# Attention logits from a shared ring of PSUM banks, two key tiles at a time

## The chip, the core and the metric

The kernel runs on one core of a Trainium2 chip. Five engines work in parallel, each through its own queue in order: TensorE (PE, matmuls, with PEld for the weight loads), VectorE (DVE), ScalarE (ACT), GpSimd (POOL) and SyncE (SP, which here only issues transfers). Matmuls write to PSUM[...]. The metric is the device time of one execution in microseconds (us); lower is better.

## The reference

The input is x, 8 images of 512 channels and 32 x 32 pixels, in float32. There are two residual layers. The second is a masked 1 x 1 convolution after a group norm. The first, which holds nearly all the work, is:

```python
t = cbs(x, cv1_w, cv1_bn, 0)                      # group norm before; 1x1 conv, batch norm, silu
ys = [t[:, :C], t[:, C:]]                         # C = 256
for i in range(2):
    z = cbs(ys[-1], m_cv1_w[i], m_cv1_bn[i], 1)   # 3x3 conv
    q, k, v = 1x1 conv of z                       # 4 heads of 64 channels, 1024 pixels
    logits = einsum('bhdi,bhdj->bhij', q, k + r) * 64 ** -0.5
    z = einsum('bhij,bhdj->bhdi', softmax(logits), v)
    ys.append(ys[-1] + silu(bn(conv1x1(z))))
x = x + cbs(concat(ys), cv2_w, cv2_bn, 0)
```

So each of 8 images passes twice through an attention over 1024 queries and 1024 keys with 4 heads.

## The kernel before

The attention is cut into 64 **units**: 8 images x 2 blocks x 2 pairs of heads (`hp`) x 2 halves of 512 queries. A unit has eight **key tiles** of 128 keys (`t`). Keys lie on the partitions, queries along the columns, and the two heads of a pair are the two halves of a [128, 2, 512] tile.

For each unit (class `Unit`, from line 412):

- `logits(t)` (L421): two matmuls, one per head, with 64 rows each (TensorE's tile 64*128), into the pair of banks `lg` of the pool `ps_l`; ACT copies the pair to `st` in one instruction of 1024 columns (L432); DVE keeps the running maximum `mx` (L436, L438).
- `top()` and `spread()` (L440, L449): transposes that turn the maxima into one negated maximum per query, spread over all partitions in `mb` (pool `ps_m`, two banks).
- `soften(t)` (L456): DVE adds `mb` to `st` (L458), ACT takes the exponential in place (L461), POOL sums the tiles (L464, L466).
- `values(t)` (L468): two matmuls, one per head, into 64 columns each (tile 128*64), accumulated over the eight tiles in `po` (pool `ps_o`, one bank).
- `finish()` (L480): denominators by a matmul with ones (L484, also 128*64), a reciprocal (L486) and a product (L487).

Units overlap: while unit u runs `soften` and `values`, the logits of the next unit, `nxt`, are computed, tile by tile. All else (3 x 3 and 1 x 1 convolutions, projections to q, k and v, norms) is written as generators, **fillers**, which yield after some two matmuls. Their results, and those of `top` and `finish`, go to single banks from `bank()` (L69), three of them in the pool `ps_f`. Eight banks in all: two for logits, two for `mb`, one for `po`, three for the rest.

The program order is set by the loop over **slots** of four units (one image and block): after each step of a unit, `advance(share)` (L886) runs fillers until a share of the slot's filler work is done. `slot_filler` (L781) lists this work with estimated times; what the next slot needs must be done after 0.74 of the steps. `clock.tick` adds estimates for the unit's own matmuls, which set only when delayed fillers (norms) are let in. A slot has 4 x 10.5 steps: per unit one after `top`, one after `spread`, eight tiles, and half a step after the last values. A list scheduler of the framework then places the instructions on each engine, by program order among those that it takes to be ready; pools hand out whichever buffer is free. So instructions can stand in another order than written.

The hand-written order within a unit is: `top`, fillers, `finish` of the unit before, `spread`, fillers; then per tile t: on even t from 2, the values of t-2 and t-1; the logits of the next unit's tile t; `soften(t)`, whose addition on DVE stands behind the next unit's maximum through a dependency that fixes only the order (`behind`); fillers. At the end the last two values.

Ten buffers of `st` (pool `stp`) hold the tiles of both units.

Of the kernel before, what the change touches and what calls it, by code (L numbers as in the profile page):

```python
# [17 lines left out]
ALU = mybir.AluOpType  # L18
AX = mybir.AxisListType
PSUM = bass.MemoryType.PSUM  # L20
IN_ORDER = mybir.DependencyInfo(mybir.DependencyClass.NoSync, mybir.DependencyReason.DATA)

P = 128
# [5 lines left out]
HALF = 512  # L29
# [3 lines left out]
KT = 8  # L33
# [6 lines left out]
def conv_preact_kernel(ctx: ExitStack, tc: tile.TileContext, x, cv1, cv2, mcv1, qkv, mcv2, bn, rw, rh, conv, s_in, t_in, out):  # L40
    nc = tc.nc
    stt = nc.vector.scalar_tensor_tensor

    def pool(name, bufs, **kw):
        return ctx.enter_context(tc.tile_pool(name=name, bufs=bufs, **kw))
# [12 lines left out]
    gr = pool("gr", 2)  # L58
    tp = pool("tp", 3)
    wt = pool("wt", 3)  # L60
    ps_l = pool("ps_l", 1, space=PSUM)
    ps_m = pool("ps_m", 1, space=PSUM)
    ps_o = pool("ps_o", 1, space=PSUM)
    ps_f = pool("ps_f", 3, space=PSUM)

    def pair(p, tag, name):
        return p.tile([P, 2, HALF], F32, tag=tag, name=name)

    def bank(name):  # L69
        return ps_f.tile([P, HALF], F32, tag="bank", name=name)  # L70
# [4 lines left out]
    def flat(t):  # L75
        return t.rearrange("p a b -> p (a b)")

    def load(dst, src):
        nc.sync.dma_start(out=dst, in_=src)  # L79
# [97 lines left out]
    class Image:  # L177
# [221 lines left out]
        def last(self, h, xn):  # L399
            n = self.n  # L400
            for cp in range(2):
# [6 lines left out]
                    nc.vector.tensor_tensor(res[:, c], ps, res[:, c], ALU.add)  # L408
                load(out[n, cp, :, :, ts(h, HALF)], res)


    class Unit:
        def __init__(self, im, i, hp, half):
# [7 lines left out]
        def logits(self, t):  # L421

            if t == 0:
                self.begin()
            lg = pair(ps_l, "lg", f"lg_{self.name}_{t}")
            for h in range(2):
                r = slice(HD * h, HD * h + HD)
                nc.tensor.matmul(  # L428
                    lg[:, h], self.k[r, ts(t, P)], self.q[r, self.hp, ts(self.half, HALF)], start=True, stop=True
                )  # L430
            st = pair(stp, "st", f"st_{self.name}_{t}")
            nc.scalar.copy(flat(st), flat(lg))  # L432
            self.st.append(st)
            if t == 1:
                self.mx = pair(one, "mx", f"mx_{self.name}")
                return nc.vector.tensor_tensor(flat(self.mx), flat(self.st[0]), flat(lg), ALU.max)  # L436
            elif t > 1:
                return nc.vector.tensor_tensor(flat(self.mx), flat(self.mx), flat(lg), ALU.max)  # L438

        def top(self):  # L440

# [11 lines left out]
                for c in range(4):  # L453
                    nc.tensor.transpose(self.mb[:, h, ts(c, P)], self.nm[:, h, c : c + 1].to_broadcast([P, P]), ident)  # L454

        def soften(self, t, behind=None):  # L456
            st = flat(self.st[t])
            add = nc.vector.tensor_tensor(st, st, flat(self.mb), ALU.add)  # L458
            if behind is not None:
                tc.add_manual_dep(add.ins, behind.ins.name, IN_ORDER, reason="maximum first")  # L460
            nc.scalar.activation(st, st, AF.Exp)  # L461
            if t == 1:
                self.acc = pair(one, "acc", f"sum_{self.name}")
                nc.gpsimd.tensor_tensor(flat(self.acc), flat(self.st[0]), st, ALU.add)  # L464
            elif t > 1:
                nc.gpsimd.tensor_tensor(flat(self.acc), flat(self.acc), st, ALU.add)  # L466
# [162 lines left out]
    units = [Unit(im, i, hp, half) for im, i in slots for hp in range(IT) for half in range(2)]  # L629
# [25 lines left out]
    clock = Clock()  # L655
# [118 lines left out]
    bg = Background()  # L774
# [6 lines left out]
    def slot_filler(s):  # L781

        prev = slots[s - 1] if s else (None, 0)
        nxt = slots[s + 1] if s + 1 < len(slots) else (None, 0)
        todo, needed = [], 0.0

        def add(us, g):
            nonlocal needed
            todo.append((us, g))
            needed += us  # L790

        im, i = nxt
        if im and i == 0:
            add(0.0, call(im.load_y))
        add(8.0, bg.take(8.0))
        if im and i == 1:
            add(7.0, im.conv_m2(0))
            add(9.0, bg.take(9.0))
        if prev[1] == 1:
            add(7.0, prev[0].conv_m2(1))  # L800
            add(0.0, call(lambda: bg.add(*(cls(prev[0], h) for cls in (Second, Last) for h in range(2)))))
        if im:
            add(32.0, im.conv3(i))
            add(7.0, bg.take(7.0))
            add(21.0, im.project(i))
        rest = SHARE - needed if im else 1e3
        if rest > 0:
            todo.append((rest if im else 84.0, bg.take(rest, wait=True)))
        total = sum(c for c, _ in todo)
        return needed, total, todo  # L810
# [37 lines left out]
    first, second = images[:2]  # L848
# [13 lines left out]
    positions(1)  # L862
    clock.run(bg.take(7.0, force=True))
    clock.run(first.project(0))
    for t in range(KT):
        units[0].logits(t)
        clock.run(bg.take(3.4))

    before = None
    for s in range(len(slots)):  # L870
        needed, total, todo = slot_filler(s)
        state = {"done": 0.0}

        def filler():
            for us, g in todo:
                start = state["done"]
                for cost in g:
                    clock.tick(cost)
                    state["done"] += cost
                    yield  # L880

                state["done"] = max(state["done"], start + us)

        fill = filler()

        def advance(share):  # L886
            goal = max(share * total, min(1.0, share / 0.74) * needed + 0.1)
            while state["done"] < goal:
                if next(fill, "end") == "end":
                    break  # L890

        steps = 4 * (KT + 2.5)
        for j in range(4):
            u = units[4 * s + j]
            nxt = units[4 * s + j + 1] if 4 * s + j + 1 < len(units) else None
            base = j * (KT + 2.5)
            u.top()
            clock.tick(0.9)
            advance((base + 1) / steps)
            if before:  # L900
                before.finish()
            u.spread()
            clock.tick(1.8)
            advance((base + 2) / steps)
            for t in range(KT):
                if t and t % 2 == 0:
                    u.values(t - 2)
                    u.values(t - 1)
                    clock.tick(2.0)
                top = None  # L910
                if nxt:
                    top = nxt.logits(t)
                    clock.tick(1.05)
                u.soften(t, top)
                advance((base + 3 + t) / steps)
            u.values(KT - 2)
            u.values(KT - 1)
            clock.tick(2.0)
            advance((base + KT + 2.5) / steps)
            before = u  # L920
        for _ in fill:
            pass
# [57 lines left out]
```

## Time and profile before

| what | value |
|---|---|
| time, median of 3 runs | 3639.33 us (3638.44 to 3651.5) |
| profiled execution, its own time | 3646.37 us |
| its span, first to last instruction | 3644.7 us |
| mean granted TensorE clock | 0.979 |
| busy PE / DVE / ACT / POOL | 93% / 57% / 47% / 32% |
| attention loop, first logits to last values | about 216 to 3540 us |

"L428" is line 428 of the kernel before. A row of a group gives engine, operation, output<-inputs, shapes, count, busy us and mean ns of one, then the idle time of the engine before them and what ended it. One matmul of the program in float32 appears as two in the profile, each with its weight load (PEld). 64*128, 128*64 and 128*128 are the part of the array that a matmul uses, rows by columns. Starts of weight loads show when the array took the next matmul; durations of matmuls overlap.

### The profile page before, as it was taken

The numbers are of one execution on the slowest core, as the hardware profiler recorded it, in microseconds if no ns is written. First come the engines' busy times: TensorE is split into PE (matmuls) and PEld (weight loads), VectorE is DVE, ScalarE is ACT, GpSimd is POOL, SyncE is SP. The second block draws the span as 40 slices with busy tenths as digits, with TensorE's granted clock in tenths as the row PEclk, the third lists the DMA queues.
The fourth block names the chain that finished last, engine by engine and source line by source line (L and its number), as shares of the span: only waits on it lengthen the run. The fifth ranks groups of instructions, "written<-read, shape, count | busy, mean of one in ns | idle before, by whom it ended". The sixth has DMA issues, their size and how long they took to land. (4 is left out here: it accounts for less than half of the span.)

```text
span 3644.7 us, 31236 instructions
## 1 busy us (share of the span) xinstructions
PE 3381.1 (93%) x11716; PEld 1464.6 (40%) x11716; DVE 2064.8 (57%) x2141; ACT 1722.7 (47%) x1801; POOL 1149.6 (32%) x523
## 2 busy tenths in 40 slices
PE   6899989998999999989999999989999999999988
PEld 3644334343434334343434344343434344343333
DVE  4435565465656565665656565665655565655542
ACT  3045764645454544534454534544455534544531
POOL 1003233233333323333333333333333323333330
PEclk9899999999999999999999999999999999999989
DMA  7652341320222241422223241423223141513345
GB/s 279 211 182 96 100 154 64 115 96 24 98 81 102 75 142 52 155 82 97 94 81 106 71 142 52 160 77 118 73 90 112 62 144 49 167 52 108 103 153 173
DMA packets 142279, 400.21 MB, mean 110 GB/s; under 512 B 13104, under 2 KB 14384, under 8 KB 142128
## 3 DMA queue, kind: packets, MB, share of 16 engines
q1 hardware_dynamic: 141408, 397.99, 32.7%
q8 instruction: 92, 1.51, 0.2%
q14 instruction: 59, 0.48, 0.0%
q10 hardware_dynamic: 720, 0.23, 0.0%
HBM read 318.47 MB, written 79.69 MB: 109 GB/s over the span
## 5 line engine op out<-in xcount | busy, mean ns | idle before, releaser
L466 POOL TENSOR_TENSOR sum<-sum,st 128x1024 f32<-128x1024 f32 x384 | 913.1, 2378 | 1143.2 <-ACT st L461 1140.6
L461 ACT ACTIVATE st<-st 128x1024 f32<-128x1024 f32 x512 | 540.3, 1056 | 882.3 <-DVE st L458 880.2
L438 DVE TENSOR_TENSOR mx<-mx,lg 128x1024 f32<-128x1024 f32 x384 | 468.1, 1219 | 783.6 <-ACT st L432 783.6
L432 ACT COPY st<-lg 128x1024 f32<-128x1024 f32 x512 | 512.8, 1001 | 428.9 <-PE lg L428 301.5
L428 PE MATMUL lg<-q,k 64*128 64x512 f32 x2048 | 614.5, 647 | 101.7 <-DVE mx L438 94.5
L472 PE MATMUL po<-st,v 128*64 128x512 f32 x2048 | 570.4, 631 | 72.3 <-ACT st L461 70.1
L458 DVE TENSOR_TENSOR st<-st,mb 128x1024 f32<-128x1024 f32 x512 | 618.9, 1210 | 4.8 <-PE mb L454 4.8
L241 PE MATMUL m<-plane,w_m 128*128 128x256 f32 x2304 | 574.2, 392 | 0.6 <-DVE dd L285 0.6
L241 PEld LDWEIGHTS m<-plane,w_m 128*128 128x128 f32 x2304 | 416.3, 190 | 243.9 <-issue 191.4
L172 PE MATMUL cv<-y,w_cv 128*128 128x512 f32 x1024 | 496.1, 615 | 4.3 <-DMA y<-y 4.3
L464 POOL TENSOR_TENSOR sum<-st,st 128x1024 f32<-128x1024 f32 x64 | 153.7, 2402 | 875.3 <-ACT st L461 856.2
L428 PEld LDWEIGHTS lg<-q,k 64*128 64x128 f32 x2048 | 163.6, 186 | 435.5 <-DVE mx L438 224.3
L172 PEld LDWEIGHTS cv<-y,w_cv 128*128 128x128 f32 x1024 | 180.4, 191 | 284.3 <-issue 274.6
L486 DVE RECIPROCAL rb<-den 128x512 f32<-128x512 f32 x64 | 214.9, 3357 | 121.6 <-PE den L484 121.5
L172 PE MATMUL cv<-x,w_cv 128*128 128x512 f32 x512 | 247.5, 623 | 14.5 <-ACT x L166 14.5
L472 PEld LDWEIGHTS po<-st,v 128*64 128x64 f32 x2048 | 103.8, 136 | 383.9 <-ACT st L461 240.5
L172 PE MATMUL l<-x,w_l 128*128 128x512 f32 x512 | 246.2, 617 | 7.9 <-ACT x L166 7.9
L172 PE MATMUL qk<-z,w_qkv 128*128 128x512 f32 x512 | 249.9, 613 | 0.5 <-DVE k L325 0.5
L131 ACT ACT_TABLE_LOAD x126 | 161.7, 1283 | 14.9 <-issue 9.7
L436 DVE TENSOR_TENSOR mx<-st,lg 128x1024 f32<-128x1024 f32 x64 | 78.0, 1219 | 148.1 <-ACT st L432 148.0
L461 ACT ACT_TABLE_LOAD x124 | 159.1, 1283 | 2.2
L172 PEld LDWEIGHTS cv<-x,w_cv 128*128 128x128 f32 x512 | 94.6, 196 | 151.0 <-issue 125.6
(143 smaller groups left out, 2301.8 us busy)
## 6 DMA issues: line engine op xcount, KB each, us to landing
w_m<-w_m SPq DMA_DIRECT2D x96, 768.0 KB, 4.3
w_cv<-in_cv SPq DMA_DIRECT2D x92, 512.0 KB, 3.5
y<-y SPq DMA_DIRECT2D x64, 512.0 KB, 4.8
x<-in_x SPq DMA_DIRECT2D x56, 512.0 KB, 4.8
y<-y SPq DMA_DIRECT2D x64, 256.0 KB, 3.4
k<-r SPq DMA_DIRECT2D x32, 512.0 KB, 3.8
res<-y SPq DMA_DIRECT2D x32, 512.0 KB, 4.5
xr<-in_x SPq DMA_DIRECT2D x32, 512.0 KB, 4.1
```

The costliest lines, as they stand in the source:

```text
L131: nc.scalar.activation(dst, src, AF.Silu, bias=bn_b[:, col : col + 1], scale=bn_s[:, col : col + 1])
L172: nc.tensor.matmul(ps, w, moving, start=(n == 0), stop=(n == len(terms) - 1))
L241: nc.tensor.matmul(ps[:, ts(co, 256)].rearrange("p (t x) -> p t x", x=F), w[:, co, c, dx], u[:, 9 * c : 9 * c + 8, dx : dx + F], start=(j ...
L428: nc.tensor.matmul(lg[:, h], self.k[r, ts(t, P)], self.q[r, self.hp, ts(self.half, HALF)], start=True, stop=True)
L432: nc.scalar.copy(flat(st), flat(lg))
L438: return nc.vector.tensor_tensor(flat(self.mx), flat(self.mx), flat(lg), ALU.max)
L458: add = nc.vector.tensor_tensor(st, st, flat(self.mb), ALU.add)
L461: nc.scalar.activation(st, st, AF.Exp)
L464: nc.gpsimd.tensor_tensor(flat(self.acc), flat(self.st[0]), st, ALU.add)
L466: nc.gpsimd.tensor_tensor(flat(self.acc), flat(self.acc), st, ALU.add)
L472: nc.tensor.matmul(self.po[HD * h : HD * h + HD], self.v[:, t, ts(h, HD)], self.st[t][:, h], start=(t == 0), stop=(t == KT - 1),)
L486: nc.vector.reciprocal(rb, den)
```

## The change

- The pools `ps_l` (a pair) and `ps_f` (three banks) become one: `ps_f` with five single banks, for logits, fillers, `top` and `finish`.
- `logits(t)` takes two single banks. ACT copies each head's half apart (512 columns), and DVE takes the maximum of each half apart.
- `in_turn` chains the maxima and the additions of `soften` on DVE in exactly the written order (an order alone, no wait across engines).
- Tiles go in pairs: the values of t-2 and t-1, `soften(t)`, the next unit's logits of t and t+1, `soften(t+1)`, then fillers for two steps.
- `finish` of the unit before moves behind `spread` and its fillers, right ahead of the first pair. The half step at the end is gone: 4 x 10 steps.
- The first unit's logits, ahead of the loop, go in pairs too.

```diff
-    ps_l = pool("ps_l", 1, space=PSUM)
-    ps_f = pool("ps_f", 3, space=PSUM)
+    ps_f = pool("ps_f", 5, space=PSUM)
...
+    def in_turn(instruction):
+        if turn:
+            tc.add_manual_dep(instruction.ins, turn.pop().ins.name, IN_ORDER, reason="order of the softmax")
+        turn.append(instruction)
...
-            lg = pair(ps_l, "lg", f"lg_{self.name}_{t}")
+            lg = [bank(f"lg_{self.name}_{t}_{h}") for h in range(2)]
...
-            nc.scalar.copy(flat(st), flat(lg))
             self.st.append(st)
+            for h in range(2):
+                nc.scalar.copy(st[:, h], lg[h])
             if t == 1:
                 self.mx = pair(one, "mx", f"mx_{self.name}")
-                return nc.vector.tensor_tensor(flat(self.mx), flat(self.st[0]), flat(lg), ALU.max)
-            elif t > 1:
-                return nc.vector.tensor_tensor(flat(self.mx), flat(self.mx), flat(lg), ALU.max)
+            for h in range(2 if t else 0):
+                so_far = self.st[0] if t == 1 else self.mx
+                in_turn(nc.vector.tensor_tensor(self.mx[:, h], so_far[:, h], lg[h], ALU.max))
...
-        def soften(self, t, behind=None):
+        def soften(self, t):
             st = flat(self.st[t])
-            add = nc.vector.tensor_tensor(st, st, flat(self.mb), ALU.add)
-            if behind is not None:
-                tc.add_manual_dep(add.ins, behind.ins.name, IN_ORDER, reason="maximum first")
+            in_turn(nc.vector.tensor_tensor(st, st, flat(self.mb), ALU.add))
...
-        steps = 4 * (KT + 2.5)
+        steps = 4 * (KT + 2)
...
-            base = j * (KT + 2.5)
+            base = j * (KT + 2)
             u.top()
             clock.tick(0.9)
             advance((base + 1) / steps)
+            u.spread()
+            clock.tick(0.9)
+            advance((base + 2) / steps)
             if before:
                 before.finish()
-            u.spread()
-            clock.tick(1.8)
-            advance((base + 2) / steps)
-            for t in range(KT):
-                if t and t % 2 == 0:
+                clock.tick(0.9)
+            for t in range(0, KT, 2):
+                if t:
                     u.values(t - 2)
                     u.values(t - 1)
                     clock.tick(2.0)
-                top = None
+                u.soften(t)
                 if nxt:
-                    top = nxt.logits(t)
-                    clock.tick(1.05)
-                u.soften(t, top)
-                advance((base + 3 + t) / steps)
+                    nxt.logits(t)
+                    nxt.logits(t + 1)
+                    clock.tick(2.0)
+                u.soften(t + 1)
+                advance((base + 4 + t) / steps)
             u.values(KT - 2)
             u.values(KT - 1)
             clock.tick(2.0)
-            advance((base + KT + 2.5) / steps)
```

More of the change, by code (lines that the diff above doesn't have):

```diff
@@ L409, in last @@
                 load(out[n, cp, :, :, ts(h, HALF)], res)
+    turn = []
+    def in_turn(instruction):
+        if turn:
+            tc.add_manual_dep(instruction.ins, turn.pop().ins.name, IN_ORDER, reason="order of the softmax")
+        turn.append(instruction)
     class Unit:
@@ L428, in logits @@
                 nc.tensor.matmul(
-                    lg[:, h], self.k[r, ts(t, P)], self.q[r, self.hp, ts(self.half, HALF)], start=True, stop=True
+                    lg[h], self.k[r, ts(t, P)], self.q[r, self.hp, ts(self.half, HALF)], start=True, stop=True
                 )
             st = pair(stp, "st", f"st_{self.name}_{t}")
-            nc.scalar.copy(flat(st), flat(lg))
             self.st.append(st)
+            for h in range(2):
+                nc.scalar.copy(st[:, h], lg[h])
             if t == 1:
                 self.mx = pair(one, "mx", f"mx_{self.name}")
-                return nc.vector.tensor_tensor(flat(self.mx), flat(self.st[0]), flat(lg), ALU.max)
-            elif t > 1:
-                return nc.vector.tensor_tensor(flat(self.mx), flat(self.mx), flat(lg), ALU.max)
+            for h in range(2 if t else 0):
+                so_far = self.st[0] if t == 1 else self.mx
+                in_turn(nc.vector.tensor_tensor(self.mx[:, h], so_far[:, h], lg[h], ALU.max))
         def top(self):
@@ L864, in conv_preact_kernel @@
     clock.run(first.project(0))
-    for t in range(KT):
+    for t in range(0, KT, 2):
         units[0].logits(t)
-        clock.run(bg.take(3.4))
+        units[0].logits(t + 1)
+        clock.run(bg.take(6.8))
     before = None
@@ L899, in conv_preact_kernel @@
             advance((base + 1) / steps)
+            u.spread()
+            clock.tick(0.9)
+            advance((base + 2) / steps)
             if before:
                 before.finish()
-            u.spread()
-            clock.tick(1.8)
-            advance((base + 2) / steps)
-            for t in range(KT):
-                if t and t % 2 == 0:
+                clock.tick(0.9)
+            for t in range(0, KT, 2):
+                if t:
                     u.values(t - 2)
```

## The prediction

> **What bounds the kernel now.** I read the busy shares first, then TensorE's timeline around the attention loop, then its weight loads (their starts show when the array accepts a matmul), then the groups of the two other engines.
>
> ```profile
> PE 3381.1 (93%) x11716; PEld 1464.6 (40%) x11716; DVE 2064.8 (57%) x2141; ACT 1722.7 (47%) x1801; POOL 1149.6 (32%) x523
> ```
>
> TensorE (PE) is the bound. But 93% busy says nothing of how well the time is used, so here are TensorE's matmuls in one stretch of the loop (start, duration, line, tiles, count):
>
> ```profile
> 1119.04 1.08 PE L472 MATMUL po<-st,v 128*64 128x512 f32 x4
> 1120.05 1.56 PE L241 MATMUL m<-plane,w_m 128*128 128x256 f32 x6
> 1121.55 1.13 PE L428 MATMUL lg<-q,k 64*128 64x512 f32 x4
> 1122.61 0.70 PE L241 MATMUL m<-plane,w_m 128*128 128x256 f32 x2
> 1123.31 1.08 PE L472 MATMUL po<-st,v 128*64 128x512 f32 x4
> 1124.32 1.56 PE L241 MATMUL m<-plane,w_m 128*128 128x256 f32 x6
> 1125.81 1.13 PE L428 MATMUL lg<-q,k 64*128 64x512 f32 x4
> ```
>
> Although the program writes the values of two tiles one after the other, each tile's values (L472, tile 128*64) and logits (L428, tile 64*128) stand alone between filler matmuls of the whole array (128*128): the list order puts a filler wherever the next piece isn't ready. Logits follow each other every 4.3 us, because there is one pair of banks for them and the chain logits 1.06, copy 1.00, maximum 1.22 (3.3 us with no waits between) must run before the next. What does a switch cost? The weight loads around one logits tile:
>
> ```profile
> 1506.64 0.19 PEld L172 LDWEIGHTS cv<-y,w_cv 128*128 128x128 f32 x1 [0.24 <-issue]
> 1507.07 0.19 PEld L172 LDWEIGHTS cv<-y,w_cv 128*128 128x128 f32 x1 [0.24 <-issue]
> 1508.02 0.30 PEld L428 LDWEIGHTS lg<-q,k 64*128 64x128 f32 x4 [0.76 <-issue]
> 1509.08 0.30 PEld L172 LDWEIGHTS cv<-y,w_cv 128*128 128x128 f32 x2 [0.76 <-issue]
> ```
>
> Fillers start 0.43 us apart, but the logits come 0.95 us after the last filler: 0.52 us lost on entry. The block then takes 1.06 us (1508.02 to 1509.08). And, near the end of the trace, one of only four places where the values of two tiles run together:
>
> ```profile
> 3503.16 0.20 PEld L472 LDWEIGHTS po<-st,v 128*64 128x64 f32 x4 [0.76 <-ACT st L461]
> 3503.64 0.14 PEld L472 LDWEIGHTS po<-st,v 128*64 128x64 f32 x2 [0.29 <-ACT st L461]
> 3504.07 0.14 PEld L472 LDWEIGHTS po<-st,v 128*64 128x64 f32 x2 [0.29 <-issue]
> 3505.03 0.30 PEld L172 LDWEIGHTS l<-x,w_l 128*128 128x128 f32 x2 [0.81 <-issue]
> ```
>
> Two tiles take 1.87 us here, against 2 x 1.01 = 2.02 apart (1119.04 to 1120.05 is one). So TensorE is busy, but pays for switching.
>
> [...]
>
> **The change part by part.** Counted through the timeline of weight loads, TensorE enters one of the small tilings (logits, values, denominators) from 128*128 work 873 times in all. The entry comes 0.95 us after the last load 412 times (after a 512-column filler: +0.52), about 0.52 us after 193 times (256 columns, which run 0.21 apart: +0.31), about 0.31 us after 100 times (128 columns, 0.11 apart: +0.20); the others are mixed with waits. Mean of these 705: (412 x 0.52 + 193 x 0.31 + 100 x 0.20) / 705 = 0.42 us.
>
> *Grouping.* If the new order is kept, a unit (64 of them: image, block, head pair, half) visits the small tilings five times: denominators with the first two logits, three times two values and two logits, and the last two values. 64 x 5 = 320 entries remain, 553 go: 553 x 0.42 = 232 us.
> *Second tile of a pair.* Two values together save 2.02 - 1.87 = 0.15 us; 256 pairs: 38 us. Two logits together aren't in the trace; bounded by nothing saved (2 x 1.06) and by 0.86 for the first tile as with the values (1.92), 0 to 0.20 us a pair. I take 0.20, since the streams are the same length: 51 us. Ceiling: 232 + 38 + 51 = 321 us.
> *How much of it comes.* A pair is adjacent only if all is ready. From the start of two logits: first tile out at about 1.1, first copy 1.7, four half maxima to 1.7 + 4 x 0.69 = 4.5, the second `soften` add to 5.7, its exp to 6.8. TensorE needs that exp after 1.92 (logits) + about 5 (filler for a fifth of a unit) + 0.94 (values of the first tile) = 7.9 us. The slack of 1 us is thin: an activation-table load (1283 ns in the page, 250 in all) uses it up. And the fourth unit of each group of four gets less filler. I take three quarters: 240 us.
> *Waits.* In the loop (216 to 3540 us), gaps between weight loads beyond 0.96 us add up to 207 us. Waits for the single pair of logits banks go (94.5 us by the waits of matmuls on mx L438), waits for five shared banks and the later exps come. I leave the sum as it is; the ends are -100 and +200.
>
> *Copies and maxima by half.* The rows that price it:
>
> ```profile
> L438 DVE TENSOR_TENSOR mx<-mx,lg 128x1024 f32<-128x1024 f32 x384 | 468.1, 1219 | 783.6 <-ACT st L432 783.6
> L408 DVE TENSOR_TENSOR x2r<-l,x2r 128x512 f32<-128x512 f32 x64 | 43.9, 686 | 78.1 <-PE l L172 72.0 <-DMA x2r<-x 6.1
> L338 ACT COPY v<-v 128x512 f32<-128x512 f32 x64 | 37.4, 584 | 41.0 <-PE v L330 40.1
> ```
>
> A maximum of 1219 ns becomes two of 686: +153 ns x 448 = 69 us of DVE. A copy of 1001 ns becomes two of 584: +167 ns x 512 = 86 us of ACT. Both are hidden behind TensorE: at 3400 us DVE would be (2065 + 69) / 3400 = 63% and ACT (1723 + 86) / 3400 = 53% busy. Without that cover the worst is the 69 us. The half copies also let the maximum of one half run beside the copy of the other.
> *The order on DVE.* add, four half maxima, add: 2 x 1.21 + 4 x 0.69 = 5.2 us in one fixed chain a pair. Behind a waiting maximum stand the second add, its exp, the values, and the release of the logits banks.
> *`finish` after `spread`.* The denominators move behind eight transposes and one portion of filler. Their wait for POOL's sums (17.5 us in all) goes. But reciprocal (3357 ns) and product (678 ns) now start with the first logits of a unit and delay the maxima of tile 1 to about 0.95 + 4.0 + 1.4 = 6.4 us after the denominators begin, and its exp to about 9 us; its values are due at 0.95 + 1.92 + 5 + 0.94 = 8.8. Break even; taken as nothing, the cost if not is about 64 x 1 us.
> No DMA is issued or removed; filler DMAs move with their filler, on the same SP queue.
>
> Sum, against the profiled execution's own 3646.4 us: 3646.4 - 240 = 3406. That execution is 7 us over the median of the runs, so **3400 us**.
>
> **Rivals.**
> *A, as above*: 3270 to 3490 (all of the ceiling with 50 us fewer waits, or half of it). Chance 0.53. For it: one pair of banks spaces the logits by 4.3 us today, and the new ring spaces two tiles by about 4.5.
> *B, the order breaks up again*: the second exp is late, the list order puts fillers between the two values and between values and logits, and a quarter of the ceiling comes: 3640 - 80 = 3560 (3500 to 3615). For it: today's order keeps only four of 256 pairs of values together. Against it: the distance grows from one tile to two. Chance 0.20.
> *C, slower: fillers starve for banks.* Fillers had three banks of their own; after two logits, four of five are taken. The first comes back at 1.7 + 0.69 = 2.4 us, and a filler of two matmul terms (1.72 us) needs its second bank at 1.92 + 1.72 = 3.6. That holds with 1.2 us to spare, but a reciprocal (3.36), a 2574 ns step of the convolution (L291) or a table load with its silu (1.28 + 0.78) in front of the copy or the maximum takes more. It decides from 240 / 256 = 0.94 us of extra wait a pair; at 2.4 us (every pair hit by one reciprocal-sized delay) the time is 3400 + 256 x 2.4 = 4010, at 1.5 us 3400 + 384 = 3784. I take 3780. Against it: in the 3324 us of the loop DVE is busy 1955 us and ACT 1655. Chance 0.22.
> *D, nothing changes*: saved switches are paid back in waits one for one: 3640. Chance 0.05, of which 0.04 within 0.5%.
>
> **How the numbers follow.** Half a per cent (18 us) is about what a measurement of this kernel can tell. Faster: A 0.53 + B 0.20 + the edge of D = 0.74; same 0.04; slower 0.22. The likeliest is A: 3400. About 0.06 of A lies below 3280; above 3690 lies most of C, some 0.14. So 3280 to 3690; A's own range is 3270 to 3490.
>
> **What would show it.** Values and logits in blocks of 16 weight loads (two tiles each) in the timeline; entries near 320 and not 873; two logits in about 1.92 us; DVE and ACT up by 69 and 86 us; logits' wait for mx gone. Wrong if pairs stand apart (B), or if filler weight loads wait for mx or for copies of the logits for more than some 250 us in all (C).

## The result and the profile after

The changed kernel takes 3577.93 us (median of 4 runs, 3576.06 to 3581.82) against 3640.46 us for the kernel before on the same chip: a ratio of 0.9824, 95% interval 0.9802 to 0.9845. It is faster by 62 us. The prediction said 240 us faster; the sign was right, the size nearly four times too large.

The page's busy shares of the changed kernel (busy us, share of the span, instructions):

```profile
PE 3333.1 (93%) x11716; PEld 1569.7 (44%) x11716; DVE 2144.3 (60%) x2589; ACT 1790.1 (50%) x2337; POOL 1160.5 (32%) x523
```

The share of TensorE is the same 93%. Its timeline in a good stretch of the changed kernel (start, duration, line, tiles, count) shows that the pairs formed:

```profile
331.96 1.94 PE L478 MATMUL po<-st,v 128*64 128x512 f32 x8
333.83 1.99 PE L435 MATMUL lg<-q,k 64*128 64x512 f32 x8
335.75 5.42 PE L171 MATMUL cv<-x,w_cv 128*128 128x512 f32 x12
341.10 1.94 PE L478 MATMUL po<-st,v 128*64 128x512 f32 x8
```

Values of two tiles take 1.87 us (331.96 to 333.83), logits of two 1.92 us (333.83 to 335.75): both as predicted. Counted through the weight loads, TensorE enters the small tilings 376 times instead of 873; the prediction had 320. So the main mechanism happened, and yet most of the gain is missing. A bad stretch, all engines but SP, shows one place where it went:

```profile
1034.52 1.08 PE L490 MATMUL den<-sum,ones 128*64 128x512 f32 x4
1034.89 0.78 ACT L130 ACTIVATE cv2s<-cv,bn_b,bn_s 128x512 f32<-128x512 f32 x1
1035.53 0.30 PEld L435 LDWEIGHTS lg<-q,k 64*128 64x128 f32 x4 [0.81 <-issue]
1035.53 2.97 PE L435 MATMUL lg<-q,k 64*128 64x512 f32 x8
1035.65 3.36 DVE L492 RECIPROCAL rb<-den 128x512 f32<-128x512 f32 x1 [3.17 <-PE den L490]
1036.07 0.19 PEld L435 LDWEIGHTS lg<-q,k 64*128 64x128 f32 x1 [0.24 <-issue]
1036.50 0.19 PEld L435 LDWEIGHTS lg<-q,k 64*128 64x128 f32 x1 [0.24 <-issue]
1036.75 1.56 ACT L441 COPY st<-lg 128x512 f32<-128x512 f32 x3 [1.08 <-PE lg L435]
1037.38 0.29 PEld L435 LDWEIGHTS lg<-q,k 64*128 64x128 f32 x2 [0.70 <-ACT st L441]
1038.44 0.30 PEld L171 LDWEIGHTS cv<-y,w_cv 128*128 128x128 f32 x2 [0.76 <-issue]
```

The first tile's four loads go together (1035.53): its two heads, of 64 rows each (64*128), run side by side, as the first experiment has it (1.06 us for both, 1.06 for one alone). Of the second tile, one head runs alone (1036.07, 1036.50), and the other waits until a copy of the first tile frees its bank (1037.38; which bank a tile gets is fixed in the program). Of the five banks, the denominators' is held by the reciprocal until 1039.01, and a filler's by its silu until 1035.67. The pair takes 2.91 us (1035.53 to 1038.44) instead of 1.92.

The groups that answer to those shown of before:

```profile
L441 ACT COPY st<-lg 128x512 f32<-128x512 f32 x1024 | 536.6, 594 | 477.5 <-PE lg L435 441.3
L446 DVE TENSOR_TENSOR mx<-mx,lg 128x512 f32<-128x512 f32 x768 | 482.1, 680 | 474.7 <-ACT st L441 474.6
```

And matmul waits (us in total, times, longest): two of the kernel before, then those of the changed kernel that answer to them, and three of its fillers' waits for maxima of the logits, which set their banks free:

```profile
PE lg L428 <- DVE mx L438: 94.5, 85, 3.7
PE po L472 <- ACT st L461: 70.1, 93, 3.4
...
PE po L478 <- ACT st L467: 42.4, 35, 3.3
PE lg L435 <- DVE mx L446: 31.3, 25, 4.1
PE cv L171 <- DVE mx L446: 15.8, 10, 2.9
PE m L240 <- DVE mx L446: 14.2, 12, 4.1
PE qk L171 <- DVE mx L446: 12.3, 21, 0.6
```

Half copies and half maxima cost 594 and 680 ns as expected. The waits of logits matmuls for maxima fell from 94.5 to 31.3 us.

One thing more is in the traces, and in neither the prediction nor its sum: half clock around and after long waits. TensorE starts its last weight load before a wait at 1111.74 us and the next at 1116.89; from 1115.5 to 1122.3 us only half of its clock is granted. The matmuls around the wait, and two stretches behind it (us; busy us of PE, PEld, DVE, ACT and POOL; granted clock; share and GB/s of DMA):

```profile
1111.68 1.08 PE L478 MATMUL po<-st,v 128*64 128x512 f32 x4
1116.89 2.07 PE L435 MATMUL lg<-q,k 64*128 64x512 f32 x2 [4.13 <-DVE mx L446]
...
1117.00:1122.00 5.00, 5.00 (x9) 2.91 (x10) 4.01 (x6) 2.40 (x3) 0.00 (x0) 0.50 0.29 108
1122.60:1125.60 3.00, 3.00 (x15) 2.62 (x15) 0.00 (x0) 1.05 (x1) 0.00 (x0) 1.00 0.41 158
```

At 0.50 the fillers' weight loads (L240) start 0.427 us apart, at 1.00 they start 0.216 us apart. Between the first logits and the last values the changed kernel has 28 such stretches, the kernel before 16, and each begins in a gap of over 2 us between weight loads or within 8 us after one. Half clock in that part adds up to 157 us, against 99.

### The profile page after: what moved, and what is told of

Its sections match the earlier page's. It is cut to its first block, busy times and chain, and to the rows that moved or that the text cites. A ratio compares the mean times of both kernels' runs of the same rounds, so it can differ in the third digit from the quotient of the medians.

```text
span 3580.1 us, 32601 instructions
## 1 busy us (share of the span) xinstructions
PE 3333.1 (93%) x11716; PEld 1569.7 (44%) x11716; DVE 2144.3 (60%) x2589; ACT 1790.1 (50%) x2337; POOL 1160.5 (32%) x523
## 4 chain that ended last, share of the span: by engine, by line
PE 68%; DVE 13%; issue 7%; ACT 7%; DMA 3%; POOL 2%; SPq 0%; ACTq 0%; POOLq 0%; DVEq 0%
PE cv L171 14%; PE lg L435 11%; PE po L478 10%; PE m L240 9%; PE qk L171 6%; PE l L171 6%; PE v L329 3%; DVE mx L446 3%; DVE st L466 2%; ACT st L441 2%; ACT st L467 2%; PE m L171 2%; PE den L490 2%; PE mt L454 2%; PE mb L462 1%
## 5 line engine op out<-in xcount | busy, mean ns | idle before, releaser
L441 ACT COPY st<-lg 128x512 f32<-128x512 f32 x1024 | 536.6, 594 | 477.5 <-PE lg L435 441.3
L446 DVE TENSOR_TENSOR mx<-mx,lg 128x512 f32<-128x512 f32 x768 | 482.1, 680 | 474.7 <-ACT st L441 474.6
L435 PE MATMUL lg<-q,k 64*128 64x512 f32 x2048 | 641.0, 632 | 43.0 <-DVE mx L446 31.3
L478 PE MATMUL po<-st,v 128*64 128x512 f32 x2048 | 536.4, 621 | 51.6 <-ACT st L467 42.4
L240 PE MATMUL m<-plane,w_m 128*128 128x256 f32 x2304 | 546.4, 391 | 19.0 <-DVE mx L446 14.2
L240 PEld LDWEIGHTS m<-plane,w_m 128*128 128x128 f32 x2304 | 437.6, 194 | 157.9 <-issue 47.1
L171 PE MATMUL cv<-y,w_cv 128*128 128x512 f32 x1024 | 476.3, 607 | 12.2 <-DVE mx L446 6.9
L435 PEld LDWEIGHTS lg<-q,k 64*128 64x128 f32 x2048 | 210.5, 188 | 458.8 <-issue 298.3
L492 DVE RECIPROCAL rb<-den 128x512 f32<-128x512 f32 x64 | 214.7, 3354 | 67.0 <-PE den L490 62.2
L171 PE MATMUL qk<-z,w_qkv 128*128 128x512 f32 x512 | 235.7, 603 | 12.3 <-DVE mx L446 12.3
L455 DVE TENSOR_REDUCE nm<-mt 128x4 f32<-128x512 f32 x128 | 82.5, 684 | 152.8 <-PE mt L454 152.8
```

The lines of the kernel that those rows point to most:

```text
L171: nc.tensor.matmul(ps, w, moving, start=(n == 0), stop=(n == len(terms) - 1))
L240: nc.tensor.matmul(ps[:, ts(co, 256)].rearrange("p (t x) -> p t x", x=F), w[:, co, c, dx], u[:, 9 * c : 9 * c + 8, dx : dx + F], start=(j ...
L435: nc.tensor.matmul(lg[h], self.k[r, ts(t, P)], self.q[r, self.hp, ts(self.half, HALF)], start=True, stop=True)
L441: nc.scalar.copy(st[:, h], lg[h])
L446: in_turn(nc.vector.tensor_tensor(self.mx[:, h], so_far[:, h], lg[h], ALU.max))
L478: nc.tensor.matmul(self.po[HD * h : HD * h + HD], self.v[:, t, ts(h, HD)], self.st[t][:, h], start=(t == 0), stop=(t == KT - 1),)
```

## The experiments

Times are medians of four runs, ratios against the kernel before on the same chip in the same batch.

| kernel | us | ratio (95% interval) | entries | logits blocks, us |
|---|---|---|---|---|
| before | 3640 to 3647 | 1 | 873 | 639 |
| the change | 3577.9 | 0.9824 (0.9802-0.9845) | 376 | 697 |
| written order, 5 banks | 3589.7 | 0.9853 (0.9828-0.9878) | 322 | 719 |
| ring alone | 3623.7 | 0.9934 (0.9913-0.9955) | 741 | 733 |
| order alone | 3673.8 | 1.0077 (1.0059-1.0094) | 749 | 666 |
| 7 banks | 3466.8 | 0.9512 (0.9486-0.9537) | 345 | 590 |
| 3 weight buffers, 5 banks | 3574.0 | 0.9808 (0.9784-0.9832) | 376 | 693 |
| written order, 7 banks | 3495.7 | 0.9588 (0.9557-0.962) | 322 | 522 |
| written order, 2 pairs + 3 | 3593.6 | 0.9861 (0.9833-0.9888) | 322 | 530 |
| 7 banks, additions first | 3324.7 | 0.9116 (0.9091-0.9142) | 325 | 532 |
| 5 banks, additions first | 3545.1 | 0.9716 (0.9692-0.974) | 370 | 689 |
| old loop, 2 pairs + 3 | 3673.0 | 1.0069 (1.0043-1.0095) | 783 | 725 |
| 5 banks, denominators early | 3547.2 | 0.9717 (0.9688-0.9746) | 429 | 665 |
| 7 banks, additions first, denominators early | 3313.2 | 0.9082 (0.9068-0.9095) | 388 | 531 |
| 5 banks, both | 3535.2 | 0.9681 (0.9659-0.9702) | 409 | 666 |

The batches differ by a few us, so runs of different batches are best compared by their ratios. Entries are counted in TensorE's order. "Logits blocks" is the time from the first weight load of each run of logits to the next load of anything else, summed over the trace; a wait of whatever comes behind a block counts in. Without losses I estimate it from the first experiment: 2048 loads x 0.2145 us (a quarter of the 0.858 us of a tile's streaming) plus 0.2 us at the end of each block: 546 us for before (536 blocks), 504 for the change (324 blocks).

### The price of a visit by itself

The new kernel in outline (its own code is longer; it was run once):

```diff
+ for width in (512, 256): for stage in "abcdegh": repeat 16 times
+     3 fillers; (h: logits of one head); 3 fillers
+     (e, g: values of one tile); (d, e, g: values of one tile)
+     (b, c, g: logits of one tile); (c, g: logits of one more); (h: the other head)
```

> This kernel computes none of the reference: it repeats matmul streams 16 times each, in fixed order, to price a visit to the small tilings by itself. Stages: a six fillers; b six fillers and the logits matmuls of one tile; c two tiles of logits; d values of one tile; e values of two; g values of two and logits of two; h three fillers, one head's logits, three fillers, the other head's. First with fillers of 512 columns, then of 256. Theory 1 (a visit is cheap[...]): over stage a, per repetition with 512 columns, b about 1.27 us, c 2.1, d 1.2, e 2.1, g 4.0; with 256 columns b about 1.27. Rival (the price in the prediction is right): b 1.58, c 2.44, d 1.53, e 2.39, g 4.3; with 256 columns b 1.37. For h, both heads alone: about 2.5 us, twice b, if a head alone takes as long as both together.

TensorE's timeline in stage b with fillers of 512 columns, in stage b with 256, and in stage h:

```profile
122.32 5.42 PE L58 MATMUL fwb<-xa 128*128 128x512 f32 x12
127.67 1.13 PE L58 MATMUL lg<-xa 64*128 64x512 f32 x4
128.73 5.42 PE L58 MATMUL fwb<-xa 128*128 128x512 f32 x12
...
862.78 1.13 PE L58 MATMUL lg<-xa 64*128 64x512 f32 x4
863.84 2.86 PE L58 MATMUL fnb<-xa 128*128 128x256 f32 x12
866.63 1.13 PE L58 MATMUL lg<-xa 64*128 64x512 f32 x4
...
770.79 1.12 PE L58 MATMUL lg<-xa 64*128 64x512 f32 x2
771.85 2.84 PE L58 MATMUL fwh<-xa 128*128 128x512 f32 x6
774.62 1.12 PE L58 MATMUL lg<-xa 64*128 64x512 f32 x2
```

A repetition of stage b is 6.41 us (122.32 to 128.73). Fillers' loads alone start 0.429 us apart, twelve take 5.15. So a logits tile in between costs 1.26 us, not 1.58. Likewise, over the fillers: two tiles of logits 2.12, values of one 1.21, of two 2.07, values of two and logits of two 3.98, and in stage h 2.50, each as theory 1 had it. With 256 columns a repetition of b is 3.85, its twelve fillers 2.59 (0.216 each): again 1.26. The weight loads show where the difference lies: the first load of the fillers comes 0.95 us after the last logits load, but the second only 0.11 us later, not 0.43. The trace shows these times and not the reason for them. The kernel before agrees without this experiment: in its trace, entries without a long wait come 0.42 us late on average, as the prediction counted, and the second load after a block comes 0.20 us ahead of the regular spacing.

For the streaming of a tile of four loads I take 0.858 us, two spacings of the fillers (2 x 0.429); a second tile adds as much, of logits (2.12 - 1.26 = 0.86) and of values (2.07 - 1.21 = 0.86). With v for a visit, l and w for the end of a block of logits or values: v + l = 1.26 - 0.86 = 0.40, v + w = 0.35, v + l + w = 3.98 - 3.43 = 0.55. So v = 0.20, l = 0.20, w = 0.15 us.

Stage h tells the other price: one head alone takes 1.06 us (770.79 to 771.85), as long as both heads together (127.67 to 128.73). A tile whose heads stand apart between fillers costs 2.50 instead of 1.26.

### What the prediction assumed, in full

Every matmul and transpose of TensorE goes through this:

```diff
+    def pe(instruction):
+        if pe_turn:
+            tc.add_manual_dep(instruction.ins, pe_turn.pop().ins.name, IN_ORDER, reason="written order")
+        pe_turn.append(instruction)
```

> The changed kernel with every TensorE matmul of the loop held to the written order (order alone). TensorE then enters the small tilings 322 times and the two heads of a tile never stand apart, which is what the prediction assumed in full. Prediction's prices: 320 us under the kernel before, near 3325, if the waits stay at some 207 us. Theory 1 (entry worth 0.2 us, and not 0.42): 110 + 89 = 200 us, so 3440 with unchanged waits, and later by whatever waits grow since nothing may step forward; I expect 3440 to 3560. Theory 2 (the order is irrelevant, the gain came from five banks): like the changed kernel, 3580.

3589.7 us: no faster than the list order (3577.9), above theory 1's range, and near theory 2's number, though not for its reason. With 322 entries and 256 blocks of two tiles, the logits blocks take 719 us, 229 over their price: 125 of these lie inside the blocks, and 103 pass before the filler behind a block can start. Gaps between weight loads, from the first logits to the last values, exceed 0.96 us by 270 us in all, against 207 in the changed kernel. Perfect pairs are worth little while banks aren't free.

### Ring alone, order alone

For the first, the loop of the kernel before with the new `logits`; for the second, the new loop with

```diff
-    ps_f = pool("ps_f", 5, space=PSUM)
+    ps_f = pool("ps_f", 3, space=PSUM)
+    ps_l = pool("ps_l", 1, space=PSUM)
...
-            lg = [bank(f"lg_{self.name}_{t}_{h}") for h in range(2)]
+            lg = pair(ps_l, "lg", f"lg_{self.name}_{t}")
```

and full-width copies and maxima.

> Five single shared banks, copies and maxima by head and the fixed DVE order, but the loop of the kernel before, tile by tile (TensorE order: 741 entries against 873 before and 376 after). Theory 1 (the gain is the fewer visits): 132 entries by 0.2 us less, more tiles with their heads apart (78 against 27), so 3610 to 3660. Theory 2 (the gain is the ring, no longer waiting for one pair): about 3580.

> The new loop in pairs of tiles with the old banks: one pair for logits, three for fillers, copies and maxima at full width (TensorE order: 749 entries). Theory 1: the pairs can't form with one pair of banks, 124 entries by 0.2 us less, 3600 to 3640. Theory 2 (the ring is the gain): 3640. If it is at 3580, the new places of the additions and of the denominators are what counts, and neither ring nor visits.

The ring alone gains 0.7%, in theory 1's range: its logits blocks are the longest of the table (733 us; 78 tiles have their heads apart in the order, against 27 before and 54 in the changed kernel). The order alone loses 0.8%, which no theory had. Its matmul waits, with one pair of banks under a loop that asks for two:

```profile
PE lg L436 <- DVE mx L446: 112.5, 72, 4.9
PE mt L454 <- DVE mx L446: 34.9, 19, 3.3
```

Neither part does what both do together. 55 of its tiles have their heads apart in the order, although both share a pair of banks: it is the list order that parts them there.

### Seven banks

```diff
-    wp = pool("wp", 4)
+    wp = pool("wp", 3)
...
-    ps_m = pool("ps_m", 1, space=PSUM)
...
-    ps_f = pool("ps_f", 5, space=PSUM)
+    ps_f = pool("ps_f", 7, space=PSUM)
...
-            self.mb = pair(ps_m, "mb", f"mb_{self.name}")
+            self.mb = pair(one, "mb", f"mbs_{self.name}")
             for h in range(2):
+                mb = bank(f"mb_{self.name}_{h}")
                 for c in range(4):
-                    nc.tensor.transpose(self.mb[:, h, ts(c, P)], ...)
+                    nc.tensor.transpose(mb[:, ts(c, P)], ...)
+                nc.scalar.copy(self.mb[:, h], mb)
```

> The changed kernel with seven banks in the ring: the spread maxima go through two ring banks into SBUF (two ACT copies of 584 ns a unit), which frees their two banks; three weight buffers instead of four pay for the space. The list order has 345 entries (376 with five banks). Theory 1 (with five banks the second head's logits wait for a bank of their own, and the two heads, which else run side by side, run one after the other; the logits blocks took 697 us, 193 over the price of the separate streams): the blocks fall by 100 us or more and the time to 3440 to 3500. Rival (banks aren't short; what is lost is lost to the late exponentials): 3560 to 3600.

> Control for the run with seven banks: the changed kernel with three weight buffers and five banks; TensorE's order is the same. All theories: 3575 to 3600.

3466.8 us against 3574.0 for the control: two more banks are worth 107 us, with 345 entries against 376 (the way of the spread maxima through SBUF comes with them and was not run by itself). The logits blocks fall from 693 to 590 us, by 103: 73 us inside them, 45 at the fillers behind them, while waits of values behind them grow by 18. This is theory 1's case, with the fillers' own waits for banks as a second part of it. Elsewhere the time between blocks falls by 55 us and that of the denominators by 12, while the values blocks grow by 61, so it is by chance that the 103 and the 107 are so close. What grows are values waiting for exponentials (seven banks):

```profile
PE po L479 <- ACT st L468: 124.4, 86, 3.8
PE po L479 <- DVE q L494: 16.6, 14, 3.2
```

against 42.4 us in the changed kernel.

> Seven banks and every TensorE matmul in the written order: 322 entries, heads never apart in the order. Theory 1: logits blocks near their price (some 500 us against 719 with five banks in the written order), waits for exponentials stay or grow by some 70 us: 3400 to 3470. Rival (lost to late exponentials, not to banks): 3560 to 3600, as with five banks in the written order.

> Seven banks split: two pairs for the logits of two tiles, full-width copies and maxima, three single banks for fillers, and the written order. Both heads of a tile share one pair, so neither waits alone. Theory 1: logits blocks near 500 us; fewer banks can be lent between logits and fillers, DVE and ACT are 155 us less busy: 3400 to 3480. Rival (sharing one ring matters): clearly slower than the written order with seven single banks, by over 40 us.

In the written order, seven banks bring 3589.7 down to 3495.7; the logits blocks come to 522 us, near their price, and the values' waits for exponentials rise to 178.6 us. That is a little above theory 1's range and well under the rival's. Split into two fixed pairs and three filler banks, the same seven banks give 3593.6: the logits blocks are as good (530 us), but 98 us are lost elsewhere. The values blocks are the same too (703 us against 701), so most of it, 87 us, lies between the blocks, among the fillers: gaps of over 0.96 us take 68 us more over the regular spacing there, and loads at half clock 15 more. A part are waits of fillers for the results of others to leave the three banks, in rows which the run with one ring doesn't have:

```profile
PE qk L419 <- DVE k L324: 15.1, 14, 1.5
PE m L419 <- ACT m2s L130: 14.2, 7, 2.9
```

So sharing one ring matters, as the rival to that run had it; these two rows are 29 us, and the rest is spread over smaller ones.

### The additions first

```diff
                 u.soften(t)
+                u.soften(t + 1)
                 if nxt:
                     nxt.logits(t)
                     nxt.logits(t + 1)
                     clock.tick(2.0)
-                u.soften(t + 1)
```

> Seven banks, and both additions of a pair ahead of its logits' maxima on DVE. Theory 1 (with banks enough, what remains are the values waiting for exponentials that stand behind four half maxima; 124 us of matmul waits on the exponential with seven banks): the second exponential comes some 2.8 us sooner, the waits fall by 60 us or more, 3370 to 3420. Rival (ACT itself is late, busy with copies and table loads): 3450 to 3480.

> The changed kernel (five banks) with both additions of a pair ahead of the maxima. The additions hold the logits banks 1.2 us longer. Theory 1 (banks are what is short with five): little or nothing, 3550 to 3600, and logits blocks as long as before or longer. Rival (the late exponential is the main loss in the changed kernel too): under 3520.

With seven banks: 3324.7 us, 142 us less, more than theory 1 said. The matmuls' waits on the exponential, of seven banks with additions first:

```profile
PE po L479 <- DVE q L494: 19.3, 19, 3.8
PE po L479 <- ACT st L468: 17.0, 14, 3.0
```

From 124.4 to 17.0 us; the logits blocks fall too, to 532, since the list order now keeps 247 of the pairs whole (206 with seven banks alone). With five banks the same edit brings some 1.1% (0.9716 against 0.9824), slightly more than expected, while the logits blocks stay at 689 us: the late exponential is a second loss, beside the banks and smaller while they are short.

### More banks for the old loop

The kernel before with `ps_l` of two pairs and the maxima through SBUF.

> The kernel before, tile by tile, with a second pair of logits banks (maxima through SBUF, three weight buffers); order with 783 entries. Theory 1 (bank waits and visits both count): the waits for the one pair go (some 95 us of matmul waits), the visits stay: 3540 to 3600. Rival (more banks do all of it, pairing tiles nothing): near the 3467 of seven banks with pairs.

3673.0 us, 0.7% slower: a miss of both. The waits for the pair are all but gone (6.3 us), but they come back as waits for exponentials:

```profile
PE po L473 <- ACT st L462: 149.0, 126, 5.1
```

(70.1 before). The order falls into 783 entries with 95 tiles' heads apart. A second pair of banks alone does nothing for a loop that works tile by tile. A ring of seven single banks under the old loop was not run.

### The denominators' place

```diff
+            if before:
+                before.finish()
+                clock.tick(0.9)
             u.spread()
             clock.tick(0.9)
             advance((base + 2) / steps)
-            if before:
-                before.finish()
-                clock.tick(0.9)
```

> The changed kernel with the denominators back ahead of the spread maxima (429 entries against 376). The prediction took the move as nothing. Theory 1: 53 entries by 0.2 us and the old wait for POOL's sums, 10 to 30 us slower than the changed kernel: 3585 to 3610. If the delayed maxima behind the reciprocal cost more than that, it is faster: under 3565.

3547.2 us, 1.1% faster than the change although it has 53 entries more. The logits blocks fall from 697 to 665 us. Two causes were left: the denominators' bank, held through the reciprocal, or the reciprocal in front of the maxima on DVE.

> Seven banks, additions first, and the denominators back ahead of the spread maxima. Theory 1 (the denominators' bank, held through the reciprocal of 3.36 us, is what their late place costs with five banks): with seven banks the place doesn't matter, 3315 to 3345, or a little slower for more entries. Rival (the reciprocal in front of the first pair's maxima is the cost): 3285 to 3305.

> Five banks, additions ahead of the maxima, and the denominators back ahead of the spread maxima. Alone the two gave some 33 us each over the changed kernel. Theory 1 (they mend different things): about 3510 to 3525. Rival (both mend the first pair's late exponential): about 3545.

With seven banks and the additions first, the old place brings 3313.2 against 3324.7, by the ratios 0.3%, and the intervals touch. With five banks and the additions first it brings 3535.2 against 3545.1, again 0.3 to 0.4%, and again the intervals touch. Without the additions first, five banks gave 1.1%. So once the additions are first the place is worth the same with five banks as with seven, and these runs don't decide between the two causes. For the bank: the early place shortens the logits blocks with five banks, by 32 us and with the additions first by 22, and with seven not at all (532 and 531). For the reciprocal in front of the maxima: putting the additions first takes most of the gain away. That the bank is held while a head waits, the excerpt from 1034.52 us shows; what share of the 1.1% it has stays open, and so does whether the two reorderings add up (3535.2 lies between the two expectations). The version with seven banks, additions first and early denominators is the fastest: 0.9082 of the kernel before (0.9068 to 0.9095).

## Why the prediction was right and wrong

**Grouping** formed as foreseen: 376 entries for 320 predicted. **The step that failed first is "553 x 0.42 = 232 us"**: the visit was mis-sized. The 0.42 us is what is lost on entry, and the prediction didn't look at what is gained back on exit. Its own excerpt showed it, the two loads at 1509.08 that stand as one row. Measured, a visit costs 0.20 us, for wide and narrow fillers alike. 497 entries fewer are 99 us.

**The second tile**: 0.15 and 0.20 us a pair were right. Not all pairs are whole: logits blocks fell from 536 to 324, values blocks from 511 to 336, which is 42 + 26 us.

**"How much of it comes", three quarters**, put the shortfall down to exponentials; these cost 42.4 us of matmul waits, less than the 70.1 before, though putting the additions first did gain 1.1%. **The second step that failed is the term on waits, "waits for five shared banks and the later exps come. I leave the sum as it is"**: the waits for the shared banks got no number. The time in logits blocks over their price rose from 92 to 193 us. Inside the blocks it rose from 29 to 126 us, where a head or a tile waits for its banks (as at 1037.38) or the heads stand apart in the order (54 tiles, 27 before). Before the filler behind a block it rose from 3 to 55 us. Before values that follow directly it fell from 61 to 12 us. That the banks are at the root of it, the runs in the written order show: no heads are apart in the order there, and 229 us over the price with five banks become 32 with seven.

**Waits** of the old kind were left at 207 us, and the gaps in the loop of the changed kernel come to 207 us too, but they are others: over the whole trace those at entries fell by 55 us (75 to 20), and those between whole-array loads rose by 30 (38 to 68).

Put together from the two traces: -99 (visits) - 42 - 26 + 2 (block ends of logits, values, denominators) - 55 + 30 (waits) + 100 + 14 + 10 (logits, values and denominators over their price) = -66 us. The spans differ by 3644.7 - 3580.1 = 64.6. That it closes so well is partly chance: whole-array loads at half clock, which the sum leaves out where a gap is under 0.96 us, cost 22 us over their regular spacing before and 45 after, so a term may well be off by 20 us. Some of the long waits inside blocks stand in the last terms, so the split between waiting and running apart is not exact.

**Copies and maxima by half**: the durations add up to 95 us more for the copies (86 predicted) and 62 more for the maxima (69). DVE is at 60%, ACT at 50%, so there is room to hide them; no run prices them by themselves. The maximum of one half does run beside the copy of another: in the good stretch above, the four copies of a pair start at 335.17 us and take 2.02, and their maxima start at 335.76.

**`finish` after `spread` at nothing** was wrong: some 1% of the time. The working had the reciprocal's and the product's 4 us on DVE and called it break even, and left out that the denominators' bank is one of the five for all of the reciprocal (3354 ns). Which of the two is the larger part isn't settled.

**The rivals.** C named the right resource and half of the victims: fillers' matmuls do wait for maxima of the logits, by some 54 us (15.8 + 14.2 + 12.3 + 7.0 + 4.2, rows cv, m, qk, v, m of the waits), but this is far from C's threshold of 0.94 us a pair, 240 us. The logits' own second heads pay more. B (3560, the order breaks up) came nearer in time than A by luck, for another reason: the order largely held, but its price was half and a new loss took part of that.

## What to carry to other kernels

Price a change of TensorE's tiling over a whole cycle, from the last load before it to the first regular spacing after, not by the gap on entry: here 0.32 of 0.52 us came back after fillers of 512 columns, and 0.11 of 0.31 us after those of 256. When two matmuls run side by side, as the two heads here (1.06 us for both or for one), and each needs a bank of its own, allocate and free these so that neither starts alone; and count everything that holds a bank of a shared ring, fillers and denominators under a reciprocal (3.35 us) too. An order in pairs pays when the buffers for a whole pair are there: here a second pair of banks under the old loop (+0.7%) and the new order on the old banks (+0.8%) both lost, while the new order on a ring of seven took 4.9% off, and 8.8% with the additions put ahead of the maxima. Look at the granted clock after long waits too: here the 5.15 us between the loads at 1111.74 and 1116.89 came with half clock until 1122.3, in which the fillers' loads started 0.427 us apart and not 0.216.

## What the runs showed of the hardware

- A visit of one logits tile to its small tiling cost the same 1.26 us (0.86 of it streaming, by the estimate above) between fillers of 512 columns (0.429 us apart) and of 256 (0.216 apart) in the price experiment, though the gap on entry was 0.95 and 0.52 us.
- Two matmuls of 64 rows each took as long together (1.06 us with the switch, stage b of that experiment) as one alone (1.06 us, stage h).
- After gaps of TensorE the granted clock fell to 0.50 for 3.4 to 10.2 us: in the loop of the changed kernel with all ten gaps of over 4 us between weight loads, and with 10 of the 31 of 2 to 3 us; in that of the kernel before with three of four gaps of over 4 us. Loads of 256-column matmuls then started 0.427 us apart and not 0.216 (changed kernel, 1117 to 1122 us against 1122.6 to 1125.6).
- With the maxima in SBUF the additions of `soften` took 1288, 1354 and 1423 ns each (seven banks; with the additions first; with the denominators early too), against 1210 ns when they were read from PSUM (the kernel before); no run here tells why.
